# Fused attention and mixture-of-experts block: the last group's projections an iteration earlier, the first experts' weights and items spread over the last iterations, counts copied out of PSUM, loads in program order

## The chip, the cores and the metric

The kernel runs on one core of a Trainium2 chip. The time is the device time of one execution in microseconds. TensorE (PE in the profile; PEld is its weight load) multiplies matrices into PSUM, VectorE (DVE) and ScalarE (ACT) work elementwise and read PSUM, GpSimd (POOL) works elementwise on SBUF and issues the indirect transfers, SyncE (SP) issues most of the plain transfers. Each engine runs its own instructions in order and waits on semaphores for the others.

## The reference, cut to what matters

```
h = layernorm(x) * (1 + ca) + sa                       # x is 2 x 2048 tokens of 256
q, k, v = split(h @ Wqkv)                              # 16 heads of 64
attn = softmax(where(-128 < j - i <= 0, q k^T / 8, -max))
x = x + ga * (attn v) @ Wout
h = layernorm(x) * (1 + cb) + sb
p = softmax(h @ gate_w.T + gate_b)                     # 8 experts, the best 2 of each token
for c in range(2):                                     # CAP = 640 slots per expert and choice
    pos = running count of the tokens that chose this expert
    xbuf[expert * CAP + pos] = h                       # kept while pos < CAP
    y += p * expert_mlp(xbuf)[slot]                    # relu(x W1 + b1) W2 + b2, 256 -> 1024 -> 256
x = x + gb * y
```

The kernel puts both choices of an expert into one stretch of 1280 slots (`BUF`), with at most 640 rows of each choice (`CAP`).

## The kernel before, in words

Every product that has to be exact to float32 is made of three passes of TensorE on operands split into a high and a low part: `passes` (its matmul is L232) multiplies high by high, high by low and low by high. A split costs one operation on ScalarE, which writes the high part, and then one on VectorE, which subtracts it to get the low part: L127 for weights and slots, L299 and L300 for q, k and the attention output.

**Groups, units, iterations.** The 4096 tokens are 16 groups of 256. A group has 8 head pairs, so there are 128 units (group, head pair), written `15_3` for group 15 and pair 3. An iteration `w` of the main loop (`iteration`, L1081 to L1143, 64 of them and 3 that drain) takes two new units; four iterations make a group. It is a software pipeline: in one iteration the units of `w` get scores, masks and maximum (`scores`, `pack`, `maximum`), those of `w - 1` the rest of the exponentials and the division by their sum (`exps`, and `normalize`, whose reciprocal `rd` is on VectorE and whose product `pm` is on GpSimd), those of `w - 2` are transposed (`turn`, L576), copied out and masked on GpSimd (`unpack`, L585 to L590) and multiplied by v (`values`, L609), those of `w - 3` are multiplied by Wout into a bank of their own (`out_project`). The projections of q and k (`project_qk`, a bank `pq` each, then `part`) are made for the units of `w + 1`, that of v (`project_v`) for the group itself, at most two halves in an iteration.

**PSUM.** Of the eight banks, two hold the output projection and six are a ring named by `bank`: scores (two banks a unit), transposes, projections, `av`, and the small results of the router, among them `cnt`. When a bank is asked for, the one that was given back first in program order is taken, and a bank is given back where its last reader stands in the program. An iteration asks for twelve or thirteen.

**The close of a group.** `close(g)` is a generator. Each `next` runs it to its next `yield`, and the lists `CLOSE` and `LATE` say where: "5H" is five iterations after the group's base, at mark H. `go(w, "A")`, "B", "M", "H" and "C" are the marks of an iteration, in this order. It adds the attention output to x (L649, L650) and stores it (L651), normalizes, scales and shifts (L658, L662, L663), transposes, multiplies by the router's weights, picks the two best experts (L710 to L730), counts (L761 and L762 write `cnt`), computes the weights (L768 to L775: `sm`, `rsm`, `wt`, `wt`, `h2`), then reads `cnt` for `kept` (L790) and `rank` (L782), computes the slot (L801 to L815) and scatters the rows with four indirect transfers on GpSimd (L818). The last two groups (`late`) first ask for the total so far (L741 to L760), because the first 512 rows of experts 0 and 1 are kept free of their tokens, so that these rows can be read before the attention has ended.

**The end of the attention.** While the last iterations run, the weights of experts 0 and 1 are loaded and split piece by piece (`Expert.steps`: four pieces of 512 KB, `we` in the profile), and the first item of work of expert 0 (256 slots) is loaded, transposed and taken through its two layers (`first_item`: `tp_x`, `ph` with `hm` and `r`, `y`). The three calls of `place` say at which marks. Behind the loop come item 1 (also 256 slots of expert 0) beside what is left of the last group's close, then item 5 (512 slots of expert 1), and then all others, with branches by the true counts.

**What sets the order.** From L1146 on, the engines named in `everything` (TensorE, ScalarE, VectorE, GpSimd) run their instructions in program order until L1182. SyncE is not among them: its loads are put by a planner, which has for instance placed the load of item 1 (`xt_1`) next to that of item 0, and two of expert 0's pieces near the start of the kernel. Elsewhere the planner orders all engines, except where `keep_in_program_order` stands.

The lines that the steps below come back to:

```
        v = wl.tile([P, 512], FP, tag=f"v{t}{hf}", name=f"v_{g}_{t}_{hf}", bufs=1 + t)
        adder = nc.vector if late else nc.gpsimd
            kept.rearrange("p t k e -> p (t k e)"), cnt[:, 0:n], float(CAP), None, ALU.min
    LAST_VALUES = [[(0, 0)], [(1, 0)], [(0, 1), (1, 1)], []]
    place(experts[0].pieces, NW - 4, ["0A", "3A", "3B", "3C", "4A"])
    place(experts[1].pieces, NW, ["0B", "1A", "1C", "2A", "2C"])
    place(first, NW - 2, ["0A", *"2M 2H 2C 3A 3B 3M 3C 4A 4B".split()])
```

Of the kernel before, what the change touches and what calls it, by code (L numbers as in the profile page):

```python
# [8 lines left out]
FP = mybir.dt.float32  # L9
# [8 lines left out]
P = 128  # L18
# [10 lines left out]
def adaln_block_kernel(  # L29
# [25 lines left out]
    KC = 2  # L55
# [218 lines left out]
    def project_qk(g, p2, i):  # L274

        hh, hl = hs[g]
        slot = (g % 2) * SBT
        pq = bank(f"pq_{g}_{p2}_{i}")
        for j in range(2):
            f = slice(i * HD + (2 * p2 + j) * P, i * HD + (2 * p2 + j + 1) * P)  # L280
            passes(
                pq[:, j * TS : (j + 1) * TS],
                [
                    ((wq[:, 0, k, f], wq[:, 1, k, f]), (hh[:, k, :], hl[:, k, :]))
                    for k in range(ND)
                ],
            )
        if i == 0:
            qh = wk.tile([P, 2, TS], FR, tag="qh", name=f"qh_{g}_{p2}")
            ql = wk.tile([P, 2, TS], FR, tag="ql", name=f"ql_{g}_{p2}")  # L290
            qs[g, p2] = (qh, ql)
            src, dh, dl = pq.rearrange("p (j t) -> p j t", j=2), qh, ql
        else:
            src = pq.rearrange("p (j t n) -> p j t n", j=2, t=SBT)
            dh, dl = (kr[:, n, 2 * p2 : 2 * p2 + 2, slot : slot + SBT, :] for n in range(2))
        return dh, dl, src

    def part(dh, dl, src):
        nc.scalar.copy(dh, src)  # L299
        nc.vector.tensor_tensor(dl, src, dh, ALU.subtract)  # L300

    def project_v(g, t, hf):

        hh, hl = hs[g]
        pv = bank(f"pv_{g}_{t}_{hf}")
        f = slice(2 * HD + hf * 512, 2 * HD + (hf + 1) * 512)
        passes(
            pv,
            [
                (  # L310
                    (hh[:, k, t * P : (t + 1) * P], hl[:, k, t * P : (t + 1) * P]),
                    (wq[:, 0, k, f], wq[:, 1, k, f]),
                )
                for k in range(ND)
            ],
        )
        v = wl.tile([P, 512], FP, tag=f"v{t}{hf}", name=f"v_{g}_{t}_{hf}", bufs=1 + t)
        nc.scalar.copy(v, pv)
        vs[g, t, hf] = v

# [144 lines left out]
    def clear(i):  # L465

        for r0 in range(i * BUF, (i + 1) * BUF, CAP):
            tc.keep_in_program_order(
                nc.scalar.dma_start(
                    out=xbuf[r0 : r0 + CAP, :].rearrange("(p n) d -> p n d", p=P),  # L470
                    in_=blank.rearrange("p (a d) -> p a d", a=1).to_broadcast([P, CAP // P, ROW]),
                )
            )


# [68 lines left out]
    def exps(g, hp, tiles):  # L544

        pm, mx = pms[g, hp], mxs[g, hp]
        if (g, hp) not in dens:
            dens[g, hp] = small.tile([P, 2, SBT], FP, tag="den", name=f"den_{g}_{hp}", bufs=4)
        den = dens[g, hp]
        for i in tiles:  # L550
            h, t = divmod(i, SBT)
            nc.scalar.activation(  # L552
                pm[:, h, t, :], pm[:, h, t, :], AF.Exp, bias=mx[:, h, t : t + 1],
                accum_out=den[:, h, t : t + 1],
            )
# [79 lines left out]
    def close(g):  # L635
# [2 lines left out]
        b = g // GPB  # L638
        j0 = g * SBT
        late = g >= NG - 2  # L640
        adder = nc.vector if late else nc.gpsimd
        po, xg = pos.pop(g), xs.pop(g)

        def wide2(a):
# [51 lines left out]
        def tile2(name, n=SBT):  # L696
            return small.tile([P, n], FP, tag=name, name=f"{name}_{g}", bufs=2)
# [55 lines left out]
        if late:  # L753
# [10 lines left out]
            rhs=pref[:, j0 : j0 + SBT, :, :].rearrange("p t k e -> p (t k e)"),  # L764
            start=False, stop=True,
        )
        sm = tile2("sm")
        nc.vector.tensor_reduce(sm, ex, AX.X, ALU.add)  # L768
        rsm = tile2("rsm")
# [9 lines left out]
        def own(counts, name):  # L779

            mine = small.tile([P, SBT, KC, E], FP, tag="mine", name=f"{name}_mine_{g}", bufs=2)
            nc.vector.tensor_tensor(mine, counts, oh, ALU.mult)  # L782
            r = tile2(name, SBT * KC)
            nc.vector.tensor_reduce(r, mine.rearrange("p t k e -> p (t k) e"), AX.X, ALU.add)
            return r
# [2 lines left out]

        kept = small.tile([P, SBT, KC, E], FP, tag="kept", name=f"kept_{g}", bufs=2)
        nc.vector.tensor_scalar(  # L790
            kept.rearrange("p t k e -> p (t k e)"), cnt[:, 0:n], float(CAP), None, ALU.min
        )
        both = tile3("all")
        nc.vector.tensor_tensor(both, kept[:, :, 0, :], kept[:, :, 1, :], ALU.add)
        pos_ = own(
            both.rearrange("p t (a e) -> p t a e", a=1).to_broadcast([P, SBT, KC, E]), "pos"
        )
        rank = own(cnt[:, 0:n].rearrange("p (t k e) -> p t k e", t=SBT, k=KC), "rank")
        yield
        over = tile2("over", SBT * KC)  # L800
        nc.vector.tensor_scalar(over, rank, float(CAP), float(2 * NSLOT), ALU.is_ge, ALU.mult)  # L801
# [164 lines left out]
    def scale_of(q, n):  # L966

        o = WGT + items[q][0]
        pool = mp if q else early
        gw_ = pool.tile([P, D], FP, tag="gw", name=f"gw_{q}_{n}", bufs=6 if q else 1)  # L970
        wt = [xts[q][:, n, o + b * E : o + b * E + 1] for b in range(B)]
        tc.keep_in_program_order(nc.scalar.mul(gw_, gbr[:, 0, :], wt[0]))
        nc.vector.scalar_tensor_tensor(gw_, gbr[:, 1, :], wt[1], gw_, ALU.mult, ALU.add)
        tok = pool.tile([P, 1], I32, tag="tok", name=f"tok_{q}_{n}", bufs=7 if q else 1)
        nc.gpsimd.tensor_copy(tok, xts[q][:, n, TOK : TOK + 1].bitcast(I32))
        return gw_, tok
# [18 lines left out]
    def give():  # L995
# [26 lines left out]
    NU = NG * NP  # L1022
    NW = NU // 2
    VALUES = [[(0, 0)], [(1, 0)], [(0, 1)], [(1, 1)]]
    LAST_VALUES = [[(0, 0)], [(1, 0)], [(0, 1), (1, 1)], []]

    NORM = ["0B", "1A", "1H", "2A", "2B"]
    CLOSE = ["0H", "1A", "1B", "2H", "3H", "4A", "4B", "5H", "6A", "6C"]
    LATE = {
        NG - 3: ["0H", "1A", "1B", "2B", "2H", "3A", "3B", "3H", "3C", "3C"],  # L1030
        NG - 2: ["0H", "1A", "1B", "2A", "2H", "2C", "3A", "3B", "3M", "3C"],
        NG - 1: ["0H"],
    }
    places = {}
# [1 line left out]
    def place(work, w, at):  # L1036
        for a in at:
            places.setdefault((w + int(a[0]), a[1]), []).append(work)
# [28 lines left out]

    experts = {e: Expert(e) for e in range(2)}
    first = first_item()
    place(experts[0].pieces, NW - 4, ["0A", "3A", "3B", "3C", "4A"])  # L1070
    place(experts[1].pieces, NW, ["0B", "1A", "1C", "2A", "2C"])
    place(first, NW - 2, ["0A", *"2M 2H 2C 3A 3B 3M 3C 4A 4B".split()])

    def go(w, at):
        for work in places.pop((w, at), ()):
            next(work, None)
# [4 lines left out]
    def iteration(w):  # L1081
        g, p2 = divmod(w, NP // 2)
        if p2 == NP // 2 - 1 and g + 2 < NG:
            xs[g + 2] = load_x(g + 2)
        for i in range(2 * w - 2, 2 * w):
            if 0 <= i < E:
                clear(i)
        new, old, turned, done = pair(w), pair(w - 1), pair(w - 2), pair(w - 3)
        g1, p1 = divmod(w + 1, NP // 2)
        if turned[0]:  # L1090
            turn(*turned[0])
            unpack(*turned[0])
        if old[0]:
            normalize(*old[0])
        go(w, "A")
        if w + 1 < NW:
            q = project_qk(g1, p1, 0)
        if old[1]:
            exps(*old[1], [0])
        if w + 1 < NW:  # L1100
            part(*q)
        if turned[1]:
            turn(*turned[1])
        if old[1]:
            exps(*old[1], [1, 2])
        if turned[1]:
            unpack(*turned[1])
        if old[1]:
            exps(*old[1], [3])
        go(w, "B")  # L1110
        if w + 1 < NW:
            k = project_qk(g1, p1, 1)
        if old[1]:
            normalize(*old[1])
        if w + 1 < NW:
            part(*k)
        if done[0]:
            out_project(*done[0])
        if w < NW:
            for a in VALUES[p2] if g + 1 < NG else LAST_VALUES[p2]:  # L1120
                project_v(g, *a)
        go(w, "M")
        if done[1]:
            out_project(*done[1])
        go(w, "H")
        go(w, "C")
        for u in new:
            if u:
                scores(*u)
        if new[0]:  # L1130
            pack(*new[0])
            maximum(*new[0])
            pack(*new[1])
        if turned[0]:
            values(*turned[0])
        if new[0]:
            maximum(*new[1])
            exps(*new[0], [0, 1])
        if turned[1]:
            values(*turned[1])  # L1140
        if new[0]:
            exps(*new[0], [2, 3])

    part(*project_qk(0, 0, 1))
    everything = {mybir.EngineType.PE, mybir.EngineType.Activation, mybir.EngineType.DVE, mybir.EngineType.Pool}
    order = tc.manual_schedule(engines=everything)  # L1146
    order.__enter__()
    for w in range(NW + 3):
# [17 lines left out]
    turn_slots(1, 0)  # L1166
    second = layers(1)
    for f in range(NF + LAG + 1):
        next(last, None)
        next(second, None)  # L1170
        if f in (6, 8):
            turn_slots(5, f - 6)
    load_slots(2, 2)
# [112 lines left out]
```

## Time and profile before

| | |
|---|---|
| median of 3 runs | 1175.15 us (1174.12 to 1179.05) |
| the profiled execution | 1187.46 us |
| its span, first to last instruction | 1185.7 us |
| mean granted clock of TensorE in it | 0.966 |
| attention, steady part | about 100 to 720 us; an iteration takes 11 to 12 us |
| iteration 62 begins (first transpose of its units) | 726.27 us |
| iteration 63 begins | 737.85 us |
| item 0's last second-layer matmuls end | about 785 us |
| item 5's first matmul | 816.18 us |
| first branch by the true counts (first matmul behind it) | 857.75 us |

Times in the profile are those of one execution, counted from its first instruction. A row of a timeline gives the start, the duration, the engine and the line, output and input, and in brackets how long the engine had been idle and which instruction ended that. In a list of waits a row gives who waited for whom, the total, the number of times and the longest. Buffer numbers are left out of the names, so `av` stands for the av of any unit.

### The profile page before, as it was taken

To read this page: it belongs to the slowest core of one execution; us is meant where nothing else is said; L and a number is where in the kernel's file an instruction comes from. 1 tells how busy PE (TensorE), PEld (TensorE's weight loads), DVE (VectorE), ACT (ScalarE), POOL (GpSimd) and SP (SyncE) were. 2 spreads that over 40 slices of the span, in tenths; PEclk is the share of its full clock that TensorE was granted. 3 is DMA by queue.
4 is the path that set the end of the run, shared out by engine and by line. 5 is a ranking of instruction groups with operands and counts; after the bars stand their busy time and mean duration, and the time that the engine had idled before them with its cause. 6 is when DMAs were issued, how large, how long until landed. Compare 5 with 4: busy or idle time off the path is not lost. (4 is left out here: it accounts for less than half of the span.)

```text
span 1185.7 us, 25167 instructions
## 1 busy us (share of the span) xinstructions
PE 1092.0 (92%) x9246; PEld 1004.6 (85%) x9246; DVE 873.7 (74%) x2154; ACT 679.0 (57%) x2097; POOL 591.6 (50%) x767
## 2 busy tenths in 40 slices
PE   6799999999999989999999999678889999999995
PEld 4688888888888879889889888578879999999995
DVE  6556768778778767787787777767567877777774
ACT  4467677677766657677677677533244444444441
POOL 4235474565665554665665656533420707352524
PEclk9799999999999989999999999779989999999998
DMA  6981000010010000000000001233253434242413
GB/s 228 222 202 34 9 31 19 21 38 19 20 39 19 21 34 28 29 19 27 26 19 26 27 11 57 89 105 78 38 150 96 64 105 89 73 82 74 82 48 36
DMA packets 59571, 72.09 MB, mean 61 GB/s; under 512 B 4807, under 2 KB 51152, under 8 KB 59436
## 3 DMA queue, kind: packets, MB, share of 16 engines
q1 hardware_dynamic: 36988, 44.27, 11.9%
q0 software_dynamic: 11712, 14.79, 7.2%
q10 hardware_dynamic: 10736, 11.27, 4.2%
q8 instruction: 80, 1.31, 0.5%
q14 instruction: 55, 0.45, 0.1%
HBM read 40.11 MB, written 32.27 MB: 61 GB/s over the span
## 5 line engine op out<-in xcount | busy, mean ns | idle before, releaser
L936 ACT ACTIVATE hm<-ph,b1T 128x256 fp32r<-128x256 f32 (+2 forms) x184 | 99.0, 539 | 228.5 <-PE ph L232 196.9
L552 ACT ACTIVATE pm<-pm,mx 128x128 f32<-128x128 f32 x512 | 203.8, 401 | 44.5 <-DVE mx L538 41.5
L232 PE MATMUL pq<-hh,wq 128*128 128x256 f32 x1024 | 218.9, 297 | 5.5 <-ACT hh L268 4.4
L232 PE MATMUL ph<-xT,we 128*128 128x256 f32 (+2 forms) x1104 | 205.7, 328 | 13.4 <-PEq L1230 4.4
L586 POOL TENSOR_SCALAR_AFFINE_SELECT pT<-pT 128x512 f32<-128x512 f32 (+1 forms) x128 | 81.3, 635 | 259.0 <-ACT pT L585 258.3
L232 PE MATMUL y<-we,hm 128*128 128x256 f32 x1440 | 202.1, 285 | 7.7 <-DVE hm L938 7.6
L232 PEld LDWEIGHTS y<-we,hm 128*128 128x128 f32 x1440 | 187.3, 191 | 12.1 <-DVE hm L938 10.6
L232 PEld LDWEIGHTS ph<-xT,we 128*128 128x128 f32 x1104 | 174.6, 199 | 19.0 <-issue 7.8
L232 PEld LDWEIGHTS pq<-hh,wq 128*128 128x128 f32 x1024 | 171.5, 195 | 8.0 <-ACT hh L268 4.8
L937 DVE TENSOR_SCALAR r<-ph,b1T 128x256 f32<-128x256 f32 (+2 forms) x184 | 101.9, 563 | 76.3 <-ACT hm L936 68.8
L609 PE MATMUL av<-pT,v 128*64 128x128 f32 (+1 forms) x1472 | 128.4, 319 | 22.9 <-DVE pm L529 15.9
L562 POOL TENSOR_TENSOR pm<-pm,rd 128x512 f32<-128x512 f32 x128 | 135.0, 1055 | 28.4 <-DVE rd L560 26.4
L232 PE MATMUL pq<-hl,wq 128*128 128x256 f32 x512 | 146.5, 286 | 0.0
L528 ACT COPY pm<-sc 128x256 f32<-128x256 f32 (+1 forms) x256 | 80.8, 362 | 98.9 <-PE sc L504 60.7
L999 POOL TENSOR_TENSOR ys<-ys,gw 128x256 f32<-128x256 f32 x56 | 48.1, 965 | 178.7 <-DVE ys L989 160.8
L609 PEld LDWEIGHTS av<-pT,v 128*64 128x64 f32 x1472 | 91.5, 138 | 53.4 <-POOL h L665 18.6
L529 DVE COPY_PREDICATED pm<-within,sc 128x256 f32<-128x256 int32 (+1 forms) x256 | 95.9, 421 | 40.1 <-ACT pm L528 39.7
L1000 POOL DMA_INDIRECT out_dram<-ys,tok x60 | 98.5, 1641 | 29.9 <-issue 10.8
L504 PE MATMUL sc<-kr,qh 64*128 64x256 f32 (+1 forms) x1024 | 104.3, 294 | 6.0 <-DVE ql L300 2.9
L232 PEld LDWEIGHTS pq<-hl,wq 128*128 128x128 f32 x512 | 99.9, 195 | 0.0
L552 ACT ACTIVATION_READ_ACCUMULATOR pm<-pm,mx 128x1 f32 x512 | 98.8, 193 | 0.0
L938 DVE TENSOR_TENSOR hm<-r,hm 128x256 fp32r<-128x256 f32 (+2 forms) x144 | 94.2, 654 | 5.3
(161 smaller groups left out, 2250.6 us busy)
## 6 DMA issues: line engine op xcount, KB each, us to landing
raw_w<-in_L_ffn_W_dram SPq DMA_DIRECT2D x32, 512.0 KB, 3.8
xbuf<-blank ACTq DMA_DIRECT2D x16, 685.0 KB, 10.3
xt<-xbuf SPq DMA_DIRECT2D x8, 822.0 KB, 4.7
x<-in_L_attn_x_dram SPq DMA_DIRECT2D x16, 256.0 KB, 2.7
out_dram<-x SPq DMA_DIRECT2D x16, 256.0 KB, 2.4
xt<-xbuf SPq DMA_DIRECT2D x7, 548.0 KB, 4.2
raw_wq<-in_L_attn_Wqkv_dram SPq DMA_DIRECT2D x6, 512.0 KB, 7.8
wm<-in_L_wmod_dram SPq DMA_DIRECT2D x1, 1024.0 KB
```

The lines of the kernel that those rows point to most:

```text
L232: nc.tensor.matmul(out=out_, lhsT=a, rhs=b, start=start and n == 0 and i == 0, stop=stop and n == last and i == 2, **kw,)
L504: nc.tensor.matmul(out=sc[h][:, t, lo:], lhsT=q[r, t * P : (t + 1) * P], rhs=kr[r, (0, 1, 0)[i], hp, blk, :], start=(i == 0), stop=(i == 2),)
L528: nc.scalar.copy(pm[:, h, ts, :], blocks[:, own, :])
L529: nc.vector.copy_predicated(pm[:, h, ts, :], within.rearrange("p (a k) -> p a k", a=1).to_broadcast([P, n, P]), blocks[:, before, :],)
L552: nc.scalar.activation(pm[:, h, t, :], pm[:, h, t, :], AF.Exp, bias=mx[:, h, t : t + 1], accum_out=den[:, h, t : t + 1],)
L562: nc.gpsimd.tensor_tensor(pmv, pmv, rd.rearrange("p h (t a) -> p (h t) a", a=1).to_broadcast([P, 2 * SBT, P]), ALU.mult,)
L586: nc.gpsimd.affine_select(out=pT[:, :, t0:, 0, :], in_=own[:, :, t0:, :], pattern=[[0, 2], [0, n], [-1, P]], compare_op=ALU.is_gt, fill=0. ...
L609: nc.tensor.matmul(out=av[h * DH : (h + 1) * DH, q0 : q0 + hi - lo], lhsT=v[:, f0 + h * DH : f0 + (h + 1) * DH], rhs=pT[:, h, lo:hi], star ...
L936: nc.scalar.activation(hh[:, s], phv, AF.Relu, bias=bias)
L937: nc.vector.tensor_scalar(r[:, s], phv, bias, 0.0, ALU.add, ALU.max)
L938: nc.vector.tensor_tensor(hl, r[:, 0:W], hh, ALU.subtract)
L1000: add = nc.gpsimd.indirect_dma_start(out=of, out_offset=bass.IndirectOffsetOnAxis(ap=tok[:, 0:1], axis=0), in_=y, in_offset=None, bounds_c ...
```

## The change

- In every group's close, a new tile `counts` takes a copy of `cnt` on VectorE right after the counting matmuls, and a new `yield` follows. `kept` and `rank` read the copy. The weights (`sm` to `h2`) so move to the next step of the close (6A), and `kept` to `rank` to a new one (6B).
- The projections of q and k of the last two units' iteration (63) are made in iteration 61 instead of 62, behind those for 62; iteration 62 makes none. The halves of the last group's v are made two in iteration 60, one in 61 and one at the very start of 62. The tiles `qh`, `ql` and two of `v` get a buffer more.
- Expert 0's four splits go to 62B, 62C, 63B and 63C (before: 63A, 63B, 63C, 64A), expert 1's to 64B, 64C, 65M and 66A (before: 65A, 65C, 66A, 66C). The first item's steps go to 63H, 63S, 64B, 64H, 64V, 65B, 65H, 65V and 66A, with two new marks: S after the scores and masks, V at the end of an iteration. Before they stood at 64M, 64H, 64C, 65A, 65B, 65M, 65C, 66A and 66B.
- Group 14's scale and shift (L662, L663) go from VectorE to GpSimd.
- SyncE is named in `everything`, so its transfers stand in program order too. In the built program `b2_0` and expert 0's first two pieces are now loaded at iteration 60, and `xt_1` behind the last store of x. The clear of the slot buffer and three of the scalings by the gate lose `keep_in_program_order`.
- Beside item 1, each step takes the item's own instructions first and the last group's close second.

```diff
@@ -286,8 +286,8 @@
-            qh = wk.tile([P, 2, TS], FR, tag="qh", name=f"qh_{g}_{p2}")
-            ql = wk.tile([P, 2, TS], FR, tag="ql", name=f"ql_{g}_{p2}")
+            qh = wk.tile([P, 2, TS], FR, tag="qh", name=f"qh_{g}_{p2}", bufs=3)
+            ql = wk.tile([P, 2, TS], FR, tag="ql", name=f"ql_{g}_{p2}", bufs=3)
@@ -314,7 +314,7 @@
-        v = wl.tile([P, 512], FP, tag=f"v{t}{hf}", name=f"v_{g}_{t}_{hf}", bufs=1 + t)
+        v = wl.tile([P, 512], FP, tag=f"v{t}{hf}", name=f"v_{g}_{t}_{hf}", bufs=1 + (t or hf))
@@ -638,7 +636,7 @@
-        adder = nc.vector if late else nc.gpsimd
+        adder = nc.vector if g == NG - 1 else nc.gpsimd
@@ -764,6 +762,9 @@
             start=False, stop=True,
         )
+        counts = small.tile([P, n], FP, tag="counts", name=f"counts_{g}", bufs=2)
+        nc.vector.tensor_copy(counts, cnt[:, 0:n])
+        yield
         sm = tile2("sm")
@@ -788,14 +789,14 @@
-            kept.rearrange("p t k e -> p (t k e)"), cnt[:, 0:n], float(CAP), None, ALU.min
+            kept.rearrange("p t k e -> p (t k e)"), counts, float(CAP), None, ALU.min
...
-        rank = own(cnt[:, 0:n].rearrange("p (t k e) -> p t k e", t=SBT, k=KC), "rank")
+        rank = own(counts.rearrange("p (t k e) -> p t k e", t=SBT, k=KC), "rank")
@@ -969,7 +970,9 @@
-        tc.keep_in_program_order(nc.scalar.mul(gw_, gbr[:, 0, :], wt[0]))
+        scaled = nc.scalar.mul(gw_, gbr[:, 0, :], wt[0])
+        if q not in (0, 1, 5):
+            tc.keep_in_program_order(scaled)
@@ -1022,13 +1025,13 @@
-    LAST_VALUES = [[(0, 0)], [(1, 0)], [(0, 1), (1, 1)], []]
+    LAST_VALUES = [[(0, 0), (1, 0)], [(0, 1)], [], []]
...
-    CLOSE = ["0H", "1A", "1B", "2H", "3H", "4A", "4B", "5H", "6A", "6C"]
+    CLOSE = ["0H", "1A", "1B", "2H", "3H", "4A", "4B", "5H", "6A", "6B", "6C"]
     LATE = {
-        NG - 3: ["0H", "1A", "1B", "2B", "2H", "3A", "3B", "3H", "3C", "3C"],
-        NG - 2: ["0H", "1A", "1B", "2A", "2H", "2C", "3A", "3B", "3M", "3C"],
+        NG - 3: ["0H", "1A", "1B", "2B", "2H", "3A", "3B", "3H", "3C", "3C", "3C"],
+        NG - 2: ["0H", "1A", "1B", "2B", "2H", "2C", "3A", "3B", "3M", "3C", "3C"],
@@ -1067,9 +1070,9 @@
-    place(experts[0].pieces, NW - 4, ["0A", "3A", "3B", "3C", "4A"])
-    place(experts[1].pieces, NW, ["0B", "1A", "1C", "2A", "2C"])
-    place(first, NW - 2, ["0A", *"2M 2H 2C 3A 3B 3M 3C 4A 4B".split()])
+    place(experts[0].pieces, NW - 4, "0A 2B 2C 3B 3C".split())
+    place(experts[1].pieces, NW - 1, "0B 1B 1C 2M 3A".split())
+    place(first, NW - 2, "0A 1H 1S 2B 2H 2V 3B 3H 3V 4A".split())
@@ -1086,19 +1089,23 @@
-        g1, p1 = divmod(w + 1, NP // 2)
+
+        ahead = [divmod(i, NP // 2) for i in range(w + 1, NW if w == NW - 3 else w + 2) if i < NW]
+        if w == NW - 2:
+            ahead = []
+        if w == NW - 2:
+            project_v(g, 1, 1)
...
+        for a in ahead[1:]:
+            for i in range(2):
+                part(*project_qk(*a, i))
@@ -1142,7 +1152,7 @@
-    everything = {mybir.EngineType.PE, mybir.EngineType.Activation, mybir.EngineType.DVE, mybir.EngineType.Pool}
+    everything = {mybir.EngineType.PE, mybir.EngineType.Activation, mybir.EngineType.DVE, mybir.EngineType.Pool, mybir.EngineType.SP}
@@ -1166,8 +1177,8 @@
     for f in range(NF + LAG + 1):
+        next(second, None)
         next(last, None)
-        next(second, None)
```

## The prediction

> **What bounds the kernel.** I read the engine rows of the page first, then who makes TensorE wait, then one such wait in order of time, then the end of the attention part in stretches of 5 us.
>
> ```profile
> PE 1092.0 (92%) x9246; PEld 1004.6 (85%) x9246; DVE 873.7 (74%) x2154; ACT 679.0 (57%) x2097; POOL 591.6 (50%) x767
> PE   6799999999999989999999999678889999999995
> PEclk9799999999999989999999999779989999999998
> ```
>
> TensorE (PE) is busy in nearly every slice. The holes are the start, and slices 26 to 30 (about 740 to 890 us), where the granted clock falls too. So a saving counts where it takes TensorE's idle time away, or makes such a hole shorter. The waits of TensorE:
>
> ```profile
> PE av L609 <- DVE pm L529: 15.9, 13, 1.9
> ...
> PE tp_f L676 <- DVE h L663: 5.3, 1, 5.3
> PE cnt L761 <- DVE both L746: 4.6, 2, 2.8
> ...
> PE cnt L761 <- DVE oh L723: 1.0, 1, 1.0
> ```
>
> The first row is the largest: 15.9 us in 13 waits, one in each of groups 0 to 12, in the iteration that counts the group's choices. The timeline shows one:
>
> ```profile
> 697.75 0.39 PE L762 MATMUL cnt<-pref,ones 128*128 128x32 f32 x2
> ...
> 698.92 0.65 DVE L300 TENSOR_TENSOR kr<-pq,kr 128x512 fp32r<-128x512 f32 x1
> ...
> 699.50 0.15 DVE L768 TENSOR_REDUCE sm<-ex 128x2 f32<-128x16 f32 x1
> ...
> 699.72 1.09 PE L609 MATMUL av<-pT,v 128*64 128x256 f32 x12
> ...
> 700.46 1.04 DVE L775 TENSOR_TENSOR h<-wt,rsm 128x16 f32<-128x16 f32 x1
> ...
> 701.43 0.77 DVE L529 COPY_PREDICATED pm<-within,sc 128x256 f32<-128x256 int32 x2
> ...
> 702.00 1.09 PE L609 MATMUL av<-pT,v 128*64 128x256 f32 x12 [1.20 <-DVE pm L529]
> ```
>
> The second av finds no free PSUM bank. cnt keeps one of the six until the next iteration reads it (L790, L782), so av takes the first score bank, which is free only after the copy_predicated of 701.43, and that stood behind five small operations on VectorE.
>
> **The change, part by part.** The profiled execution took 1187.46 us (span 1185.7), 12.3 us above the 1175.15 us median; I subtract the same microseconds from both.
>
> *Counts copied out of PSUM.* The bank is free when counts is written, and the five small operations move to the next iteration. In time: the kr split ends at 699.57, the copy follows. Its nearest row, kept (128x32 from the same bank, L790), took 0.16 to 0.18 us, so the bank is free at about 699.8. The second av's turn is 699.72 + 1.09 = 700.8: 1.0 us to spare. What is late next is the following iteration's first transpose, which takes the first score bank; without the five operations its copy_predicated starts at about 699.8 and ends before the transpose's turn at 701.9. So 15.9 us go. The first av's shorter waits (L768: 1.6 us in five) precede the copy and I leave them. Added: 16 copies, 2.9 us of VectorE. Moved: sm to h2 (0.16+0.17+0.15+0.17+0.17 = 0.8 us as at 768.63) to the next A, and kept to rank (704.99 to 706.13, 1.1 us) from A to B, ahead of rd and the kr split. VectorE is 74 to 79% busy in each 100 us from 100 to 600 and idles 0.95, 0.77 and 1.52 us after 706.9 in that very iteration; that covers both. Without cover they cost 1.1 us x 16 = 18 us. Bounds: -17.5 to -8.
>
> *Loads in program order, the clear's tag.* At the start b2_0 and two 512 KB pieces of W1 leave SyncE's (SP's) queue. raw_w_0_0 was issued at 29.89, after the loads that the first scores need, and raw_w_0_1 at 87.25; nobody on TensorE waited for either. They now stand at iteration 60, about 20 us before use, against 3.8 us from issue to landing. Three small setup operations change places with splits on VectorE. -0.3 us (0 to -0.6).
>
> *Projections of the last unit an iteration earlier.* In iteration 61 TensorE gets 24 more matmuls of 128x256 (12 took 691.41 to 692.93: 2 x 1.45 = 2.9 us) and iteration 60 six of 128x512 (1.4 us); iteration 62 (726.27 to 737.85) loses both, 4.3 us. TensorE's sum is zero. The 1.02 us wait of cnt for oh (L723) goes, as 2.9 us now lie ahead of it. But iteration 62 has only 7.3 us of TensorE left, beside 10.6 us on ScalarE: v 0.6, two pT 1.1, eight exponentials 4.7, two ah 0.7, four pm copies 1.4, and the two splits of W1 put there, 2.1. So ScalarE sets its length: 10.6 - 7.3 = 3.3 us of idle TensorE, less the 1.0. Net +2.3.
>
> *Experts and first item spread.* Expert 0's splits go from iterations 63 and 64 to 62 and 63, the first layers start one iteration earlier. No work disappears. What the spreading can gain is idle time and slow clock here:
>
> ```profile
> 745.00:750.00 5.00, 1.22 (x13) 0.83 (x14) 4.93 (x8) 2.41 (x6) 2.88 (x4) 0.70 0.14 40
> 750.00:755.00 5.00, 5.00 (x30) 5.00 (x30) 3.18 (x9) 4.10 (x14) 1.93 (x4) 0.62 0.57 203
> ...
> 765.00:770.00 5.00, 2.23 (x12) 2.13 (x11) 4.14 (x17) 0.74 (x2) 2.77 (x3) 0.75 0.31 89
> 770.00:775.00 5.00, 5.00 (x28) 5.00 (x27) 1.95 (x9) 1.08 (x3) 0.00 (x0) 0.57 0.05 16
> ```
>
> (Columns: stretch, length, busy time of PE, PEld, DVE, ACT and POOL, granted clock, DMA share, GB/s.) From 725 to 785 TensorE loses 2.58, 3.21, 1.36 and 2.77 us to waits, and about 6.3 us to the clock (each stretch's busy time times one minus the clock). But VectorE is busy 45.0 of these 60 us, and its queue is in order: split 0 now stands between rd of units 2 and 3 of the last group, and waits for ScalarE, where it stands behind the last exponential. By the durations above VectorE is held there some 4 to 5 us, and with it every copy_predicated that frees a score bank. Of the 16.2 us I take a third as recovered (5 us) and half of the hold as lost (2.5 us): -2.5, which the +2.3 above all but cancels. Tail: 0, bounds -12 to +10.
>
> [...] The row: after the 2.77 us gap that ended at 767.97 the clock stood at 0.75 and 0.57, which cost 2.23 x 0.25 + 5.00 x 0.43 = 2.7 us more. [...] I take the row for this part; the 1.2 us gaps of the body left the clock at 1.00, so there only their length is saved.
>
> *Group 14's scale and shift on GpSimd.* Two operations of 0.69 us leave VectorE. [...] The row (L662 and L663 at 699.00, on POOL) says 1.19 + 1.21 = 2.4. Their price is paid by unit 5's normalization behind them on POOL, inside the tail's bounds.
>
> *After the attention.* On VectorE expert 1's last split (784.95, 1.22 us) no longer stands between the new x and its statistics: -1.2. The last group's cnt comes one layer pair later, so most of its 1.8 us wait goes. Against it: xt_1, loaded with xt_0 at 732.37, is now queued on SP behind the last x (issued at 785.06). An issue later plus 3.2 us (the 274 KB row) makes 789.5 and its transpose 790.1. Its conversion on ScalarE waited for gw until 792.80 anyway, so 2.7 us cover it; uncovered it would cost 3. The tok copies that now precede group 15's scatter on POOL wait for the same load, long landed when that scatter is ready (812.08). Taken: -1.5 (-4 to +3).
>
> **Sum:** -15.9 - 0.3 + 0 - 1.5 = -17.7: span 1168.0, profiled execution 1169.8, median **1157.5 us**.
>
> **Rivals.**
> 1. *The tail gains too* (chance 0.24). If VectorE's 45.0 us came to bind, with a tenth of waits, the 58.6 us from 726.27 to 784.84 would be 49.5: 9 us less, 1148.5. For it: the four gaps named; against it: the hold on split 0.
> 2. *Half of the bank's wait comes back* in the next iteration, as rd and the kr split stand behind kept to rank (0.07): -8 - 1.8, 1165.3. Against it: VectorE's idle time there.
> 3. *The bank is not freed earlier*, because something else holds it (0.03): only -1.8, 1173.4.
> 4. *Slower* (0.05): VectorE is held at each of expert 0's four splits. 5 us each and 3 us of slow clock behind each gap make +32: 1175.15 - 17.7 + 32 = 1189. It decides from 17.7 / 4 = 4.4 us a split. For it: one queue, two engines in series. Against it: the later splits stand behind work that waits for TensorE anyway.
>
> My forecast has 0.61: the body's waits gone, the tail about even, 1150 to 1164.
>
> **Chances and range.** A measurement tells 0.5% (5.9 us) from no change. Faster: 0.61 + 0.24 + most of rival 2 = 0.90; same: 0.05; slower: 0.05. The range runs from 1143 (rival 1 with its clock loss gone as well) to 1167 (the tail's +10).
>
> **What would show it.** The row of av waiting for DVE pm falls from 15.9 us to under 2. Iterations that count take about 10.8 instead of 12.0 us. The tp_f wait is replaced by one of tp_x for xt_1 or of ph for xT. In iterations 62 and 63 TensorE's idle time is larger than before and from 750 us on smaller. The forecast is wrong if av or the next transposes keep waiting for VectorE, or if the stretch from iteration 60 to the last y0 differs by more than 10 us.

## The result and the profile after

| | before | after | ratio, 95% interval |
|---|---|---|---|
| median beside the prediction's runs (4 and 4) | 1177.10 us | 1162.12 us (1160.61 to 1163.03) | 0.9872 (0.9842 to 0.9903) |
| second set (11 and 5 runs) | 1179.84 us | 1162.69 us | 0.9847 (0.9823 to 0.9871) |
| third set (10 and 5 runs) | 1184.11 us | 1162.91 us | 0.9811 (0.9797 to 0.9825) |
| profiled execution, its span | 1187.46, 1185.7 us | 1161.56, 1159.8 us | |

The change gains 15.0, 17.2 and 21.2 us in the three sets; 17.7 were forecast. The changed kernel takes the same time in all three, and the kernel before does not: that is taken up in the part on the prediction.

The engine rows and the slices of the changed kernel's page:

```profile
PE 1086.3 (94%) x9246; PEld 999.6 (86%) x9246; DVE 877.4 (76%) x2168; ACT 676.7 (58%) x2097; POOL 593.8 (51%) x769
...
PE   6799999999999999999999997779889999999995
...
PEclk9899999999999999999999998879989999999998
```

The work is the same (9246 matmuls). In the attention's steady part one slice rises from 8 to 9 in both rows, the 15th (about 415 to 445 us before, group 8); the others stay at 9, since a wait of 1.2 us in 12 does not show in a tenth. The list of waits shows it. Its first rows for TensorE in the changed kernel:

```profile
PE y L232 <- DVE hm L939: 6.6, 10, 1.0
PE tp_c L375 <- DVE sg L373: 6.6, 1, 6.6
PE cnt L759 <- DVE both L744: 6.0, 2, 4.4
PE tp_x L895 <- DMA xt<-xbuf: 5.5, 2, 4.8
PE ph L232 <- DVE xT L127: 4.6, 2, 2.8
```

The row of av waiting for DVE pm (15.9 us in 13) is gone, and so is the smaller one of av waiting for sm (1.6 us in five); in the two later profiles of the changed kernel 0.9 and 1.0 us of av waiting for the copy stand in its place. What leads now belongs to the start (tp_c), to the end of the attention (cnt, tp_x, ph) and to the experts (y). One counting iteration of the changed kernel in order of time, the counterpart of the one that the prediction shows:

```profile
674.64 0.66 DVE L300 TENSOR_TENSOR kr<-pq,kr 128x512 fp32r<-128x512 f32 x1
...
675.22 0.17 DVE L766 COPY counts<-cnt 128x32 f32<-128x32 f32 x1
...
675.45 0.78 DVE L527 COPY_PREDICATED pm<-within,sc 128x256 f32<-128x256 int32 x2
...
675.60 1.96 PE L607 MATMUL av<-pT,v 128*64 128x256 f32 x24
```

The two av stand together as 24 matmuls without a bracket, so without idle time between them. The copy took 0.17 us and ended 0.2 us before the first av began; the copy_predicated follows it directly, where five small operations stood before.

To see where the time went I cut the profiled executions at five places that can be found in all of them: the first transpose of iterations 8, 60 and 63, the end of item 0's last second-layer matmuls (the start of the next matmul, where that overlaps it), and the first matmul behind the first branch.

| stretch, us | before, two profiles | after, three profiles | change of the mean | forecast |
|---|---|---|---|---|
| start to iteration 8 | 115.2, 113.7 | 115.3, 114.3, 114.2 | +0.15 | -0.3 |
| iterations 8 to 59 | 587.8, 584.2 | 562.2, 562.7, 564.3 | -22.9 | -15.9 |
| iterations 60 to 62 | 34.8, 34.8 | 38.0, 38.0, 38.0 | +3.2 | +2.3 |
| iteration 63 to item 0's end | 47.0, 46.9 | 44.5, 45.1, 45.2 | -2.0 | -2.5 |
| item 0's end to the branch | 72.9, 74.6 | 70.9, 72.6, 72.8 | -1.7 | -1.5 |
| the branch to the end | 328.0, 328.9 | 328.9, 327.9, 327.9 | -0.2 | 0 |

One by one, iterations 60, 61 and 62 took 11.4, 11.8 and 11.6 us before and take 12.8, 15.0 and 10.3 after. The last half of v stands ahead of iteration 62's first transpose and is so counted with 61.

### The profile page after: what moved, and what is told of

Its sections match the earlier page's. It is cut to its first block, busy times and chain, and to the rows that moved or that the text cites. A ratio compares the mean times of both kernels' runs of the same rounds, so it can differ in the third digit from the quotient of the medians.

```text
span 1159.8 us, 25187 instructions
## 1 busy us (share of the span) xinstructions
PE 1086.3 (94%) x9246; PEld 999.6 (86%) x9246; DVE 877.4 (76%) x2168; ACT 676.7 (58%) x2097; POOL 593.8 (51%) x769
## 5 line engine op out<-in xcount | busy, mean ns | idle before, releaser
L232 PEld LDWEIGHTS ph<-xT,we 128*128 128x128 f32 x1104 | 172.3, 196 | 21.2 <-issue 6.5
L584 POOL TENSOR_SCALAR_AFFINE_SELECT pT<-pT 128x512 f32<-128x512 f32 (+1 forms) x128 | 80.9, 632 | 211.6 <-ACT pT L583 211.5
L1003 POOL DMA_INDIRECT out_dram<-ys,tok x60 | 98.1, 1634 | 33.5 <-issue 11.4
```

What stands on the lines that cost most here:

```text
L232: nc.tensor.matmul(out=out_, lhsT=a, rhs=b, start=start and n == 0 and i == 0, stop=stop and n == last and i == 2, **kw,)
L584: nc.gpsimd.affine_select(out=pT[:, :, t0:, 0, :], in_=own[:, :, t0:, :], pattern=[[0, 2], [0, n], [-1, P]], compare_op=ALU.is_gt, fill=0. ...
L1003: add = nc.gpsimd.indirect_dma_start(out=of, out_offset=bass.IndirectOffsetOnAxis(ap=tok[:, 0:1], axis=0), in_=y, in_offset=None, bounds_c ...
```

## The experiments

**The kernel before, profiled again** (no edit).

> The kernel before once more, for a second profile. Theory: the 10.4 us by which its first profile lies above the median of its timed runs (1187.5 against 1177.1) are slow clock and chance stalls, so this profile lies near 1177, its list of waits has the same row of av waiting for DVE pm (about 15.9 us in 13), and TensorE's idle time between iterations 8 and 61 stays near 22 us while the clock's loss there falls below 4.6 us. Rival: the stalls come every time and only profiling is dear; then the profile is near 1187 again.

It took 1184.93 us (the kernel before on that chip: 1182.53), so near the rival's 1187 and not the theory's 1177. The row of the bank's wait is there again, with 16.0 us in 13. Summed over windows of 2.5 us between iterations 8 and 61, TensorE was idle for 20.4 us (22.2 in the first profile), and the clock took 2.9 us (4.6). So the first profile lay high by 1.7 us of clock and 1.9 us of idle time in this stretch; it was no outlier in kind.

The clock's part was a surprise, since the prediction had put it at nothing in the body. It lies in the first group of the second sequence, group 8, whose av has 8 matmuls instead of 12 and leaves TensorE less to do beside the same VectorE work. TensorE at the end of iteration 35 in this profile, in order of time:

```profile
425.35 0.87 PE L609 MATMUL av<-pT,v 128*64 128x256 f32 x8 [0.74 <-DVE sm L768]
428.16 1.55 PE L609 MATMUL av<-pT,v 128*64 128x256 f32 x8 [1.94 <-DVE pm L529]
```

and the same stretch of the same profile in windows of 1 us (stretch, length, busy time of PE, PEld, DVE, ACT and POOL with the number of instructions, granted clock, DMA share, GB/s):

```profile
424.00:425.00 1.00, 0.61 (x9) 0.40 (x7) 1.00 (x3) 0.00 (x0) 0.77 (x2) 1.00 0.00 0
...
426.00:427.00 1.00, 0.22 (x5) 0.00 (x0) 0.96 (x2) 0.00 (x0) 1.00 (x1) 1.00 0.60 191
427.00:428.00 1.00, 0.00 (x0) 0.00 (x0) 0.61 (x4) 0.27 (x1) 0.93 (x4) 0.65 0.00 0
...
433.00:434.00 1.00, 1.00 (x8) 1.00 (x6) 0.85 (x6) 1.00 (x5) 0.44 (x1) 0.50 0.00 0
```

Within the bank's wait of 1.94 us, in a stretch that is thin anyway, the clock falls to a half and stays there for 6.8 us. Busy time times lost clock makes that about 3 us; TensorE's busy time in iterations 34 to 36 is 2.3 us longer than with the copy alone (34.6 against 32.3). All three profiles with the bank's wait (these two and the one without the copy, below) have this drop; none of the eleven without it has.

**The copy alone, on the kernel before.**

```diff
+        counts = small.tile([P, n], FP, tag="counts", name=f"counts_{g}", bufs=2)
+        nc.vector.tensor_copy(counts, cnt[:, 0:n])
+        yield
         sm = tile2("sm")
...
-            kept.rearrange("p t k e -> p (t k e)"), cnt[:, 0:n], float(CAP), None, ALU.min
+            kept.rearrange("p t k e -> p (t k e)"), counts, float(CAP), None, ALU.min
...
-    CLOSE = ["0H", "1A", "1B", "2H", "3H", "4A", "4B", "5H", "6A", "6C"]
+    CLOSE = ["0H", "1A", "1B", "2H", "3H", "4A", "4B", "5H", "6A", "6B", "6C"]
```

> The kernel before with only the copy of cnt, its new step of the close and nothing else. Theory (the prediction's sum): 15.9 us of bank wait go, so -14 to -18 us, ratio 0.985 to 0.988, the whole of what the change measured. Rival 1 (the traces of before and after, which part by 24 us up to iteration 61): -20 or more, ratio below 0.983, and the rest of the change loses some us. Rival 2 (the bank was not it): -3 or less, ratio above 0.997.

Measured: 1159.31 us against 1182.53, ratio 0.981 (0.9789 to 0.9831), so -23.2 us. Neither the theory's -14 to -18 nor its reading "the whole of what the change measured" held; the time is that of the first rival, and whether the rest of the change loses something is taken up below. Iterations 8 to 59 took 563.1 us in the profile (before 587.8 and 584.2), 4.3 us of them idle and none at a lower clock. The counting iterations fell from 12.0 to 10.6 us.

**The changed kernel without the copy.**

```diff
-        counts = small.tile([P, n], FP, tag="counts", name=f"counts_{g}", bufs=2)
-        nc.vector.tensor_copy(counts, cnt[:, 0:n])
-        yield
...
```

> The changed kernel without the copy: kept and rank read cnt itself and the step behind it is gone; all else as changed. Theory: within 3 us of the kernel before (1174 to 1180), with the row of av waiting for DVE pm back at 14 to 17 us in 13 waits. Rival 1 (the rest of the change gains too): 1168 or less. Rival 2 (the rest loses and the copy hides it): 1181 or more.

1181.15 us against 1182.53, ratio 0.9987 (0.9976 to 0.9998). The time lies above the 1174 to 1180 that I gave, because the kernel before took 1182.53 on this chip; beside that, the theory holds. The first row of its list of waits:

```profile
PE av L607 <- DVE pm L527: 16.2, 13, 1.9
```

The wait is back within 0.3 us of before, with the same number and the same longest. All else that was changed is worth 0.1% without the copy.

**The changed kernel with the old end of the attention**: `LAST_VALUES`, the projections and the three `place` lines as before.

```diff
-    LAST_VALUES = [[(0, 0), (1, 0)], [(0, 1)], [], []]
+    LAST_VALUES = [[(0, 0)], [(1, 0)], [(0, 1), (1, 1)], []]
...
-    place(experts[0].pieces, NW - 4, "0A 2B 2C 3B 3C".split())
-    place(experts[1].pieces, NW - 1, "0B 1B 1C 2M 3A".split())
-    place(first, NW - 2, "0A 1H 1S 2B 2H 2V 3B 3H 3V 4A".split())
+    place(experts[0].pieces, NW - 4, ["0A", "3A", "3B", "3C", "4A"])
+    place(experts[1].pieces, NW, ["0B", "1A", "1C", "2A", "2C"])
+    place(first, NW - 2, ["0A", *"2M 2H 2C 3A 3B 3M 3C 4A 4B".split()])
```

> The changed kernel with the last group's projections, the experts' splits and the first item's steps where the kernel before has them. Theory: the tail is even, so within 3 us of the changed kernel (1159 to 1165). Rival 1 (the spreading gained 9 us as the first rival of the prediction says): 1169 to 1173. Rival 2 (it cost something): 1157 or less. In the trace the stretch from iteration 61's first transpose to item 0's last second-layer matmul was 69.7 us in the changed kernel and 70.4 in the kernel before.

1160.42 us, ratio 0.9809 (0.9789 to 0.9828): even with the copy alone on the same chip (0.981), and as fast as the changed kernel elsewhere. From iteration 61 to item 0's end it took 69.5 us, and from iteration 60 on 80.9, where the changed kernel takes 82.5 to 83.2. The 9 us of the first rival are not there.

**The changed kernel again.**

> The changed kernel once more, beside the kernel before on the same chip. The copy alone gave 0.981 (interval 0.979 to 0.983). Theory: the rest of the change (tail, order of loads, end) is worth nothing within 3 us, so ratio 0.979 to 0.984. Rival 1 (the rest loses, as the first comparison of 0.987 against 0.981 would have it): 0.985 to 0.989. Rival 2 (it gains): 0.976 or less.

1162.69 us against 1179.84, ratio 0.9847 (0.9823 to 0.9871): at the edge between the theory and its first rival.

**Only the projections back, and only the placing back**, each on the changed kernel (the parts of the diff above).

> The changed kernel with only the last group's projections where the kernel before has them (q and k of iteration 63 in 62, v as before). Theory (the prediction's +2.3 for the move): iteration 61 is 3 us shorter and iteration 62 has no idle TensorE behind ScalarE, so 1 to 3 us faster than the changed kernel. Rival: the move was needed by the spreading, and without it iteration 62 or 63 grows by 3 us or more: slower by 2 us or more.

> The changed kernel with only the experts' splits and the first item's steps at their old marks, the projections moved as in the change. Theory (the prediction's -2.5 for the spreading): iteration 62 has less to do for ScalarE but TensorE idles in iterations 63 to 66, so 1 to 4 us slower than the changed kernel. Rival 1 (the hold of VectorE behind ScalarE is what counts): 2 us or more faster. Rival 2: no difference within 1.5 us.

1161.73 and 1161.17 us, ratios 0.9847 (0.9823 to 0.9872) and 0.984 (0.9816 to 0.9865) beside 0.9847 for the changed kernel in the same set. Neither part can be told from nothing by its time: the first is 1.0 us faster than the changed kernel, at the near edge of its theory, and the second 1.5 us faster, against its theory of 1 to 4 slower. The traces say what each does to iterations 60 to 62, which took 34.8 us before and take 38.0 in the changed kernel. With the new projections and the old placing they take 36.2: the projections cost 1.4 us, for the half of v moved into iteration 60 lengthens it by 1.4, and iterations 61 and 62 stay at 23.4 together although they lose that work. With the old projections and the new placing they take 36.5: the splits put into iteration 62 cost 1.7. From iteration 63 to item 0's end the old placing takes 47.0 us, as before, and the new one 45.7 with the old projections and 44.5 to 45.2 in the changed kernel, so the splits give some 2 us back there. Iteration 61 and iteration 62 in the changed kernel:

```profile
690.28:705.23 14.95, 14.95 (x134) 13.74 (x133) 12.88 (x48) 9.44 (x34) 8.70 (x11) 1.00 0.08 27
705.23:715.52 10.29, 7.14 (x69) 5.63 (x67) 6.45 (x10) 7.17 (x23) 8.05 (x9) 0.84 0.42 137
```

(Columns as in the windows above.) Iteration 62 has 7.14 us of TensorE and 3.15 us of idle time here; in the two later profiles it is just as long, with 6.3 us of TensorE and 4.0 idle, so the clock of 0.84 filled idle time. ScalarE is busy for 7.17 us of the 10.29. The timeline of the changed kernel shows what sets the length:

```profile
709.06 1.99 ACT L127 CAST we<-raw_w 128x1024 fp32r<-128x1024 f32 x2
...
710.14 1.25 DVE L127 TENSOR_TENSOR we<-raw_w,we 128x1024 fp32r<-128x1024 f32 x1 [3.75 <-ACT we L127]
...
712.65 1.97 PE L607 MATMUL av<-pT,v 128*64 128x256 f32 x12 [2.20 <-POOL pT L588]
...
715.04 0.76 DVE L527 COPY_PREDICATED pm<-within,sc 128x256 f32<-128x256 int32 x2
...
715.52 0.48 PE L574 MATMUL tp<-ident,pm 128*128 128x128 f32 x1 [0.90 <-DVE pm L527]
...
716.56 0.40 ACT L550 ACTIVATE pm<-pm,mx 128x128 f32<-128x128 f32 x1 [4.16 <-DVE mx L536]
```

VectorE stands still for 3.75 us before split 0, for ScalarE's half of it; rd (711.32), split 1 (713.06 to 715.12), the two copy_predicated (715.04) and with them the next transposes come late behind it. Then the roles turn: ScalarE has nothing to do for 4.16 us and waits for VectorE's maximum. The wait of av for GpSimd (2.20 us) is the longer gap of TensorE, but av is done 0.9 us before the transposes can start, so VectorE sets the length.

**SyncE left to the planner**, all else as changed.

```diff
-    everything = {mybir.EngineType.PE, mybir.EngineType.Activation, mybir.EngineType.DVE, mybir.EngineType.Pool, mybir.EngineType.SP}
+    everything = {mybir.EngineType.PE, mybir.EngineType.Activation, mybir.EngineType.DVE, mybir.EngineType.Pool}
```

> The changed kernel with SyncE left to the planner, as in the kernel before: the first two pieces of expert 0 and b2_0 go back near the start, item 1's slots are loaded beside item 0's. Theory (the prediction: 0.3 us at the start, and xt_1's later load covered because its conversion on ScalarE waits for item 0's scaling anyway): within 1.5 us of the changed kernel (1161 to 1164 where the kernel before takes 1177 to 1184); in the trace the wait of tp_x for the load (4.8 us) goes, and a wait of nearly the same length for tp_f or ph stands in its place. Rival: the load was the cause of the gap, so -3 to -5 us.

1162.25 us against 1181.82, ratio 0.9834 (0.9808 to 0.986): no difference. The start of item 1 in the timeline of the changed kernel,

```profile
764.83 1.12 PE L895 MATMUL tp_x<-ident,xt 128*128 128x128 f32 x4 [4.81 <-DMA xt<-xbuf]
767.47 2.16 PE L232 MATMUL ph<-xT,we 128*128 128x256 f32 x6 [1.52 <-ACT xT L127]
```

and in that of this one:

```profile
762.64 0.60 PE L895 MATMUL tp_x<-ident,xt 128*128 128x128 f32 x4
770.21 2.16 PE L232 MATMUL ph<-xT,we 128*128 128x256 f32 x6 [6.97 <-ACT xT L127]
```

With the slots there in time, the transposes run at once and the whole idle time, 6.97 us instead of 4.81 + 1.52 = 6.33, is that of the conversion on ScalarE. ScalarE in the same trace:

```profile
769.18 0.51 ACT L973 ACTIVATE gw<-gbr,xt 128x256 f32<-128x256 f32 x1 [8.99 <-POOL ys L1002]
769.59 0.57 ACT L127 CAST xT<-tp_x 128x512 fp32r<-128x512 f32 x1
```

The conversion stands behind item 0's second scaling by the gate, which has one tile with the first (`bufs=1`) and so waits until GpSimd has used the first. The late load is covered, as the prediction had it.

**Item 1 early.** On the changed kernel, both causes of that gap are taken away: the slots are loaded beside item 0's, the two scalings get the place of a v tile that is no longer needed, and item 1's transposes and split go ahead of the last group's normalization.

```diff
+        load_slots(1)
...
-        gw_ = pool.tile([P, D], FP, tag="gw", name=f"gw_{q}_{n}", bufs=6 if q else 1)
+        if q:
+            gw_ = pool.tile([P, D], FP, tag="gw", name=f"gw_{q}_{n}", bufs=6)
+        else:
+            if n == 0:
+                scales["pair"] = wl.tile([P, 2 * D], FP, tag="v10", name="gw_0", bufs=2)
+            gw_ = scales["pair"][:, n * D : (n + 1) * D]
...
-    next(last)
...
-    load_slots(1)
...
     turn_slots(1, 0)
+    next(last)
...
-        next(last, None)
+        if f:
+            next(last, None)
```

> The changed kernel with item 1's slots loaded beside item 0's, both of item 0's scalings by the gate in tiles of their own, and item 1's transposes and split ahead of the last group's normalization (whose following steps come one layer pair later). Theory: in the changed kernel TensorE idles 4.8 and 1.5 us at 760.0 to 767.5, for the load issued at 760.55 and then for ScalarE, and the clock is at 0.5 for some 8 us behind it; the transposes now start at once, so -4 to -8 us against the changed kernel. Rival 1 (VectorE, which has x, ys, the scalings and the split in its queue there, takes the place of the load): -1 to -3. Rival 2 (the last group's later close delays the branch): 0 or slower.

1159.35 us beside 1162.69 for the changed kernel, ratios 0.982 (0.9796 to 0.9844) and 0.9847: -3.3 us, just short of the theory's -4 to -8. Its timeline:

```profile
760.31 0.60 PE L895 MATMUL tp_x<-ident,xt 128*128 128x128 f32 x4
761.58 0.39 PE L232 MATMUL ph<-xT,we 128*128 128x256 f32 x1 [0.68 <-ACT xT L127]
763.76 2.71 PE L232 MATMUL ph<-xT,we 128*128 128x256 f32 x11 [1.79 <-DVE xT L127]
```

Of 6.3 us of idle time 2.5 are left, and the second of these waits is VectorE's, as its first rival said.

**Once more side by side: the copy alone, the change, and the copy with item 1 early** (the last is the kernel before with the two diffs; the load of item 1's slots is left where its planner puts it).

> The kernel before with only the copy of cnt, once more, now beside the changed kernel on the same chip. Theory (from the first two sets: 23.2 us less than before for the copy alone, 17.1 us for the whole change): the rest of the change costs 2 to 5 us, so this is 2 to 5 us below the changed kernel of this set. Rival: the sets differ by their chips alone, and both agree within 1.5 us here.

> The changed kernel beside the copy alone on the same chip. Theory: 2 to 5 us above it, and in the traces the difference lies between the first transpose of iteration 61 and the first matmul behind the first branch (140.1 us in the copy alone, 140.6 and 142.9 in the changed kernel so far). Rival: within 1.5 us of it.

> The kernel before with the copy of cnt and the earlier start of item 1 (both of item 0's scalings in tiles of their own, item 1's transposes and split ahead of the last group's normalization, whose further steps come one layer pair later). Theory: in the copy alone TensorE idles 5.4 and 1.6 us at 759 to 767 and runs at half clock for about 8 us behind it; as in the changed kernel with item 1 early this stretch becomes some 5 us shorter, so -3 to -6 us against the copy alone. Rival: what is gained there is waited for at item 5 or at the branch: -1 or less.

1161.99, 1162.91 and 1158.48 us against 1184.11; ratios 0.9795 (0.9777 to 0.9813), 0.9811 (0.9797 to 0.9825) and 0.977 (0.9747 to 0.9794). The copy alone and the whole change agree within 1 us, so the 2 to 5 us that I expected the rest to cost are not there. The copy with item 1 early has the lowest median of all; its interval lies just below that of the change. Against the copy alone it is -3.5 us, within the theory, but its runs spread from 1154.61 to 1162.09 and the two intervals overlap, so that gain is not shown on this kernel. It gives part of its gain back at item 5, whose conversion on VectorE comes behind the last group's 17 small operations for its slots. TensorE and VectorE there, in its timelines:

```profile
788.70 4.63 PE L232 MATMUL ph<-xT,we 128*128 128x512 f32 x10 [3.04 <-DVE xT L127]
```

```profile
787.88 0.17 DVE L838 CAST fill<-total 128x8 int32<-128x8 f32 x1
787.96 0.68 DVE L127 TENSOR_TENSOR xT<-tp_x,xT 128x512 fp32r<-128x512 f32 x1
```

## Why the prediction was right, and where it was off

*The bank.* Right in mechanism, place and cure: the wait is there without the copy (16.2 us in 13) and gone with it, in either kernel. The term was too small: against the -15.9 of the sum, iterations 8 to 59 lost 22.9 us between the two profiles before and the three after, and the copy alone gained 23.2 and 22.1 us on two chips. The idle time there fell from 21.3 to 4.2 us on the average, -17.1: most of the 1.6 us of the first av's waits, which I left in because they precede the copy, went too. The clock's loss fell from 3.9 to 0.6 us, -3.3: "the 1.2 us gaps of the body left the clock at 1.00, so there only their length is saved" was read off one group and does not hold in group 8. The last -2.5 us is recorded busy time, and why it fell is not shown. Of the cover that I named, VectorE's idle time behind the moved operations, nothing ran out: no wait came up in the next iteration, so the bound of -8 and the second rival fall.

*The start.* -0.3 was forecast, and the profiles scatter by 1.5 us there. Not settled, and too small to matter.

*Projections and spreading.* The tail was forecast at 0, with +2.3 for iterations 60 to 62 and -2.5 behind them; the stretches measured +3.2 and -2.0. Both parts cost something, 1.4 us by the projections and 1.7 by the splits, where I had put all under the projections. Iteration 62 was to be 10.6 us long by ScalarE's work, with 3.3 us of idle TensorE; it took 10.3 with 3.15 to 4.0. That match is in part luck: ScalarE worked only 7.17 us there, and the length was set by VectorE, held by split 0 and then at work on split 1. The hold itself I had named, at 4 to 5 us and under the spreading; it measured 3.75. The wait of cnt for oh (1.02 us), said to go, is indeed missing in the changed kernel and is back with the old projections.

*After the attention.* -1.5 forecast, -1.7 measured. The load of item 1's slots is covered by ScalarE's chain, as argued. The scalings' single tile, named as the cover, turned out to be the better thing to mend.

*The rivals.* The tail does not gain 9 us: from iteration 60 to item 0's end the changed kernel takes 1.2 us more than before. The bank was what held av. The slower case saw its mechanism, but at two splits of eight: VectorE waited 3.75 and 3.74 us for ScalarE there, the first at the price of +1.7 us in iteration 62, far from four times 8.

*The total.* The forecast of 1157.5 us was made from a median of 1175.15, and the changed kernel takes 4.6 us more; the difference, -17.7, lies between the measured -15.0, -17.2 and -21.2. That it comes so close is in part luck. The largest term was 7 us too small, and the profiles' own sum is -23.5 (from 1184.4 to 1160.9 in the means), because the two profiles before lie above all medians of that kernel. Those medians go from 1177.1 to 1184.1 by set, while the changed kernel's stay within 0.8 us. The clock does not explain the sets: within each, the slower runs of the kernel before tend to have the lower mean granted clock (in the second set 0.970 to 0.973 up to its median of 1179.84 us, 0.968 or 0.969 above), but it averages 0.970 in the second set and in the third, whose medians lie 4.3 us apart. They ran on different chips; what it is there that slows this kernel and not the changed one stays open.

Not tried by themselves: group 14's scale and shift on GpSimd, and the order beside item 1. Without the copy they and all the rest are worth the 0.1% above.

## What to carry to other kernels

- In this kernel a PSUM bank is held until its last reader, however small that reader is and wherever a later step puts it: `kept` and `rank`, whose reads of cnt took 0.16 and 0.18 us an iteration later, made av wait 13 times, 15.9 us in all. A copy of 0.17 us to SBUF gave the sixth bank back to the pipeline and was worth 23.2 and 22.1 us on two chips, more than the rearranged end of the attention, which moved waits from one iteration to another.
- When a wait of the main engine names a releaser, look at what that releaser frees and who else holds one: the row said VectorE and copy_predicated, and the cure was in the router's counts.
- Before a load is moved earlier, follow its first consumer: item 1's slots could come in time, which took away a wait of 4.8 us, without effect, because the engine that converts them stood behind a tile with one buffer.

## What was unexpected of the hardware

TensorE's clock fell to a half without any long gap, and the traces show what went before. In each of the 14 profiles all drops begin whole multiples of 3.413 us apart and, but for the last one at the end of the kernel, last such multiples: the changed kernel's drops at 408.42, 712.21 and 725.86 us last 3.41, 6.83 and 3.41 us and are 303.79 and 13.65 us apart, 89 and 4 times 3.413. I cut all profiles from 100 us on to 20 us before their ends into stretches of that length, counted from a drop, and took the 4096 stretches at full clock. Of the 97 in which TensorE was busy for less than half, 93 were followed by half clock; of the 3855 with 0.75 or more, none; of the 144 between, 9. In the first profiles of the two kernels alone, these are 15 of 15, none of 546 and 1 of 24 (busy for 0.61). So in these profiles the drop goes with the thin stretch rather than with a single gap.

In iteration 35 it matters how these stretches lie over the work. At its start the eleven profiles without the bank's wait have the same waits, the longest of 1.25 us; five show a drop of 3.4 us there and six show none. The changed kernel in two executions, first its first profile and then its second, cut in the same way:

```profile
401.59:405.01 3.42, 2.82 (x36) 2.18 (x34) 3.21 (x13) 2.14 (x7) 1.45 (x4) 1.00 0.00 0
405.01:408.42 3.41, 1.52 (x12) 0.99 (x12) 2.65 (x7) 0.53 (x2) 0.94 (x1) 1.00 0.23 77
408.42:411.83 3.41, 3.34 (x15) 3.34 (x16) 2.70 (x9) 1.89 (x9) 0.00 (x0) 0.50 0.02 5
```

```profile
402.45:405.86 3.41, 1.91 (x20) 1.14 (x16) 3.31 (x10) 0.36 (x1) 1.28 (x2) 1.00 0.02 5
405.86:409.28 3.42, 2.38 (x17) 2.02 (x18) 2.29 (x8) 0.81 (x4) 0.00 (x0) 1.00 0.22 77
409.28:412.69 3.41, 3.31 (x25) 2.98 (x26) 2.70 (x8) 3.41 (x15) 0.46 (x2) 1.00 0.00 0
```

In the first, one stretch holds most of the thin part and TensorE is busy for 1.52 of 3.41 us; in the second two share it, with 1.91 and 2.38. The thinnest stretch is busy for 0.40 to 0.48 in the five with the drop and for 0.56 to 0.59 in five of the six without; the sixth, at 0.48, kept its clock.

These drops cost no time: iterations 34 to 36 take 35.97 to 36.11 us with one and 35.99 to 36.11 without, and TensorE is idle for 0.2 us of iteration 35 instead of 1.0. The slow clock filled a wait that was there anyway. The drop of 6.8 us that began in the bank's wait ran on into iteration 36, where two of its three profiles show TensorE without any idle time left.
